# A selective scan with its sum over states: the products h*C moved between engines, and the scan written in place

## The chip, the cores and the metric

The kernel runs on one core of one Trainium2 chip. The metric is the device time of one execution in microseconds (us), from the first to the last instruction; the time of a kernel is the median of several runs. The engines are TensorE (PE, with its weight loads as PEld), VectorE (DVE), ScalarE (ACT), GpSimd (POOL), and SyncE (SP), which issues the transfers. Each has its own queue of instructions, and they meet at semaphores.

## The reference

Eight images of 56 x 56 tokens with 192 channels go through two layers, each added to its input. The first layer is a group norm, depthwise convolutions for q, k and v, and softmax attention with three heads. The second is a group norm and a selective scan in four directions (along rows, along columns, and both reversed). The change touches the scan alone:

```python
delta = jax.nn.softplus(dts + dt_projs_bias[None, :, :, None])

def step(h, inp):
    u_l, d_l, B_l, C_l = inp
    dA = jnp.exp(d_l[..., None] * A)
    dBu = d_l[..., None] * B_l[:, :, None, :] * u_l[..., None]
    h = dA * h + dBu
    y = jnp.sum(h * C_l[:, :, None, :], axis=-1)
    return (h, y)
...
_, ys = jax.lax.scan(step, h0, inputs)
```

For each image and direction the scan runs over 3136 tokens. It has 384 channels (Din), and each channel has 16 states, each with its own A, B and C. B and C belong to a token and a state and are the same for all channels. y sums h*C over the 16 states.

## The kernel before

A direction is cut into 7 chunks of T = 448 tokens, so that there are 8 x 4 x 7 = 224 chunks, each with 16 states. The channels lie on the 128 partitions in NJ = 3 blocks; a tile of one state and one chunk is 128 x 3 x 448. Constants and pools of buffers:

```python
BY_DVE = (0, 6, 11)
BY_POOL = (3, 8, 13)
...
    s1 = ctx.enter_context(tc.tile_pool(name="s1", bufs=1))
    s2 = ctx.enter_context(tc.tile_pool(name="s2", bufs=2))
    s3 = ctx.enter_context(tc.tile_pool(name="s3", bufs=3))
    s4 = ctx.enter_context(tc.tile_pool(name="s4", bufs=4))
    py = ctx.enter_context(tc.tile_pool(name="py", bufs=1, space=PSUM))
    pa = ctx.enter_context(tc.tile_pool(name="pa", bufs=2, space=PSUM))
    pb = ctx.enter_context(tc.tile_pool(name="pb", bufs=3, space=PSUM))
...
    def bank(name):
        return pb.tile([128, 512], F32, name=name, tag="bank")
```

The three banks of `pb` are shared by nearly all that TensorE writes, the attention and the convolutions too; `da` has two banks of its own, `y` three.

What a chunk needs ahead of its scan (delta as `dl`, delta times u as `du`, the C of each token as a column, `ct`) is prepared while the chunk before it runs:

```python
...
        pct = bank("pct")
        ct = s2.tile([TP, SUB, NST], F32, name="ct")
        nc.scalar.copy(ct, pct[:TP, :SUB * NR].rearrange("p (s r) -> p s r", r=NR)[:, :, R + NST:NR])
        st["ct"] = ct

        dl = s2.tile([128, NJ, T], F32, name="dl")
        e = s1.tile([128, NJ, T], F32, name="e")
        ln = s1.tile([128, NJ, T], F32, name="ln")
        for j in range(NJ):
            pdt = bank("pdt")
            nc.tensor.matmul(pdt[:, :T], dtws[k][:, j * 128:(j + 1) * 128], xd[0:R, :], start=True, stop=True)
            q = k * NJ + j
            nc.scalar.activation(e[:, j], pdt[:, :T], AF.Abs, bias=dtb[:, q])
            nc.scalar.activation(dl[:, j], pdt[:, :T], AF.Relu, bias=dtb[:, q])
            yield st
        nc.scalar.activation(e, e, AF.Exp, scale=-1.0)
        nc.scalar.activation(ln, e, AF.Identity, bias=one)
        nc.vector.scalar_tensor_tensor(e, ln, -1.0, e, ALU.add, ALU.subtract)
        nc.scalar.activation(ln, ln, AF.Ln)
        nc.vector.tensor_tensor(dl, dl, e, ALU.subtract)
        nc.vector.tensor_tensor(dl, dl, ln, ALU.add)
        du = s2.tile([128, NJ, T], F32, name="du")
        nc.gpsimd.tensor_tensor(du, dl, xs, ALU.mult)
        st["dl"], st["du"] = dl, du
        yield st
```

The loop over the states of a chunk:

```python
        y = py.tile([128, NJ, 512], F32, name="y")
        newc = s2.tile([128, NJ, NST], F32, name="newc")
        done = []
        for n in range(NST + 1):
            if n < NST:
                bb = s4.tile([128, T], F32, name="bb")
                nc.sync.dma_start(bb, rows[n, :].partition_broadcast(128))
                cm = None
                if n in BY_DVE:
                    cm = bank("cm")
                    nc.tensor.matmul(cm[:, :T], sel[:, BY_DVE.index(n), :], xd, start=True, stop=True)
                elif n in BY_POOL:
                    cm = s2.tile([128, T], F32, name="cb")
                    nc.sync.dma_start(cm, rows[NST + n, :].partition_broadcast(128))
                dbu = s3.tile([128, NJ, T], F32, name="dbu")
                nc.gpsimd.tensor_tensor(
                    dbu, du, bb.unsqueeze(1).to_broadcast([128, NJ, T]), ALU.mult)
                h = s4.tile([128, NJ, T], F32, name="h")
                for j in range(NJ):
                    da = pa.tile([128, 512], F32, name="da")
                    nc.scalar.activation(da[:, :T], dl[:, j], AF.Exp,
                                         scale=acoef[:, k * NJ + j, n:n + 1])
                    nc.vector.tensor_tensor_scan(
                        h[:, j, rev], da[:, 0:T][:, rev], dbu[:, j, rev],
                        0.0 if ci == 0 else carry[:, j, n:n + 1], ALU.mult, ALU.add)
                nc.scalar.copy(newc[:, :, n:n + 1], h[:, :, last])
                done.append((n, h, cm))
            if n >= 1:
...
```

`dbu` is delta*u*B by GpSimd; `da` is exp(delta*A) by ScalarE, in a PSUM bank; VectorE scans along the tokens, three instructions a state, from `da` and `dbu` into `h`; ScalarE copies the last column for the next chunk. Then h*C is added to `y` in one of three ways:

```python
    def add_state(n, h, cm, y, ct):

        if n in BY_DVE:
            nc.vector.tensor_tensor(h, h, cm[:, :T].unsqueeze(1).to_broadcast([128, NJ, T]), ALU.mult)
        elif n in BY_POOL:
            for j in range(NJ):
                nc.gpsimd.tensor_tensor(h[:, j], h[:, j], cm, ALU.mult)
        if n in BY_DVE or n in BY_POOL:
            for j in range(NJ):
                nc.tensor.matmul(y[:, j, :T], ident, h[:, j], start=(n == 0), stop=(n == NST - 1))
            return

        for s in range(SUB):
            cols = slice(s * TP, (s + 1) * TP)
            ht = bank("ht")
            for j in range(NJ):
                nc.tensor.transpose(ht[:TP, j * 128:(j + 1) * 128], h[:, j, cols], ident)
            g = s3.tile([TP, DIN], F32, name="g")
            nc.scalar.activation(g, ht[:TP, :DIN], AF.Copy, scale=ct[:, s, n:n + 1])
            for j in range(NJ):
                nc.tensor.matmul(y[:, j, cols], g[:, j * 128:(j + 1) * 128], ident[:TP, :TP],
                                 is_transpose=True, start=False, stop=(n == NST - 1 and s == SUB - 1))
```

States 0, 6 and 11: VectorE multiplies by C, which TensorE has spread over the partitions (`cm`), and TensorE adds to `y` by a matmul with the identity. States 3, 8 and 13: GpSimd multiplies, by C rows that a transfer has spread (`cb`). The ten others: TensorE transposes blocks of 112 tokens to a bank `ht`, so that C lies along the partitions and is a scale of a ScalarE copy (`g`), and transposes back, adding in `y`.

Between the states the loop interleaves other work: `finish`, the output projection of the image before, in the chunks of direction 0; and `front`, the first layer and the second layer's convolution of the image to come, in the chunks of directions 1 to 3 (in all four for the first image). The last image has no front beside its scan.

```python
...
                slot += 1
                want = total * (slot - first_slot) / (NTOK - NST - first_slot)
                while spent < want:
                    got = next(fill, None)
                    if got is None:
                        break
                    spent += got
...
```

The program's instructions are put in a fixed order for each engine when it is built: a scheduler sets the order, by what is ready and by the program's own sequence.

Of the kernel before, what the change touches and what calls it, by code (L numbers as in the profile page):

```python
# [8 lines left out]
F32 = mybir.dt.float32  # L9
AF = mybir.ActivationFunctionType  # L10
ALU = mybir.AluOpType
# [10 lines left out]
T = 448  # L22
# [12 lines left out]
NJ = DIN // 128  # L35
NST = 16
R = 12
NR = R + 2 * NST
NDIR = 4
BY_DVE = (0, 6, 11)  # L40
BY_POOL = (3, 8, 13)
EPS = 1e-5
CAP = 60.0
NTOK = NDIR * NCH * NST
# [3 lines left out]
def kernel(  # L48
# [24 lines left out]
    nc = tc.nc  # L73
# [7 lines left out]
    def fill(name, shape, value):  # L81
        t = const.tile(shape, F32, name=name)
        nc.vector.memset(t, value)
        return t
# [5 lines left out]
    one = fill("one", [128, 1], 1.0)  # L90

    heads2 = fill("heads2", [128, 2, TP], 0.0)
    for h in range(2):
# [7 lines left out]
                            base=0, pattern=[[-6, 16], [0, 6]], channel_multiplier=1)  # L101
    nc.gpsimd.affine_select(out=gv, in_=gv, compare_op=ALU.is_ge, fill=0.0,
                            base=5, pattern=[[6, 16], [0, 6]], channel_multiplier=-1)


    sel = fill("sel", [NR, len(BY_DVE), 128], 1.0)
    for i, n in enumerate(BY_DVE):
        nc.gpsimd.affine_select(out=sel[:, i], in_=sel[:, i], compare_op=ALU.is_equal, fill=0.0,
                                base=-(R + NST + n), pattern=[[0, 128]], channel_multiplier=1)

    pwq = load("pwq", [CP, NB, C], pw_q.rearrange("(b p) d -> p b d", p=CP))
    pwkv = load("pwkv", [CP, NB, 2 * C], pw_kv.rearrange("(b p) d -> p b d", p=CP))
# [59 lines left out]
    s1 = ctx.enter_context(tc.tile_pool(name="s1", bufs=1))  # L172
    s2 = ctx.enter_context(tc.tile_pool(name="s2", bufs=2))
    s3 = ctx.enter_context(tc.tile_pool(name="s3", bufs=3))
    s4 = ctx.enter_context(tc.tile_pool(name="s4", bufs=4))
    py = ctx.enter_context(tc.tile_pool(name="py", bufs=1, space=PSUM))
    pa = ctx.enter_context(tc.tile_pool(name="pa", bufs=2, space=PSUM))
    pb = ctx.enter_context(tc.tile_pool(name="pb", bufs=3, space=PSUM))
# [2 lines left out]
    def bank(name):  # L181
        return pb.tile([128, 512], F32, name=name, tag="bank")
# [359 lines left out]
    def prepare(b, k, c, i):  # L542

        xs = s2.tile([128, NJ, T], F32, name="xs")
        nc.sync.dma_start(xs, made[b]["xcs"][k % 2][:, :, c * T:(c + 1) * T])
        if i == 0:
            dtw = s2.tile([R, DIN], F32, name="dtw")
            nc.sync.dma_start(dtw, dt_wT[:, k, :])
            dtws[k] = dtw
        yield {}  # L550
        px = bank("px")
        for j in range(NJ):
            nc.tensor.matmul(px[:NR, :T], xpw[:, k, j], xs[:, j], start=(j == 0), stop=(j == NJ - 1))
        xd = s2.tile([NR, T], F32, name="xd")
        nc.scalar.copy(xd, px[:NR, :T])
        rows = dchunk.tile([2 * NST, T], F32, name="rows")
        nc.sync.dma_start(rows, xd[R:NR, :])
        st = {"xs": xs, "xd": xd, "rows": rows}
# [4 lines that stand above are left out]
            nc.tensor.transpose(pct[:TP, s * NR:(s + 1) * NR], xd[:, s * TP:(s + 1) * TP], ident[:NR, :NR])  # L563
# [3 lines that stand above are left out]

        dl = s2.tile([128, NJ, T], F32, name="dl")
        e = s1.tile([128, NJ, T], F32, name="e")
        ln = s1.tile([128, NJ, T], F32, name="ln")  # L570
        for j in range(NJ):
            pdt = bank("pdt")
            nc.tensor.matmul(pdt[:, :T], dtws[k][:, j * 128:(j + 1) * 128], xd[0:R, :], start=True, stop=True)  # L573
            q = k * NJ + j
            nc.scalar.activation(e[:, j], pdt[:, :T], AF.Abs, bias=dtb[:, q])
            nc.scalar.activation(dl[:, j], pdt[:, :T], AF.Relu, bias=dtb[:, q])  # L576
            yield st
        nc.scalar.activation(e, e, AF.Exp, scale=-1.0)
        nc.scalar.activation(ln, e, AF.Identity, bias=one)
        nc.vector.scalar_tensor_tensor(e, ln, -1.0, e, ALU.add, ALU.subtract)  # L580
        nc.scalar.activation(ln, ln, AF.Ln)
        nc.vector.tensor_tensor(dl, dl, e, ALU.subtract)
        nc.vector.tensor_tensor(dl, dl, ln, ALU.add)  # L583
        du = s2.tile([128, NJ, T], F32, name="du")
        nc.gpsimd.tensor_tensor(du, dl, xs, ALU.mult)  # L585
        st["dl"], st["du"] = dl, du
        yield st

    def run_all(gen):
        st = None  # L590
        for st in gen:
            pass
        return st

    def add_state(n, h, cm, y, ct):

        if n in BY_DVE:
            nc.vector.tensor_tensor(h, h, cm[:, :T].unsqueeze(1).to_broadcast([128, NJ, T]), ALU.mult)  # L598
        elif n in BY_POOL:
            for j in range(NJ):  # L600
                nc.gpsimd.tensor_tensor(h[:, j], h[:, j], cm, ALU.mult)  # L601
        if n in BY_DVE or n in BY_POOL:
            for j in range(NJ):
                nc.tensor.matmul(y[:, j, :T], ident, h[:, j], start=(n == 0), stop=(n == NST - 1))  # L604
            return
# [13 lines that stand above are left out]
    total = sum(front(0))  # L619
    cur = run_all(prepare(*steps[0]))  # L620
    carry = None
    fill, spent, given = None, 0.0, 0
    es = None
    for i, (b, k, c, ci) in enumerate(steps):
        if k == 0 and ci == 0:
# [3 lines left out]
            fill = front(b + 1) if b + 1 < nb else iter(())  # L629
# [3 lines left out]
        nxt = None  # L633
        rev = slice(None, None, -1 if k >= 2 else 1)
        last = slice(0, 1) if k >= 2 else slice(T - 1, T)
        dl, du, xd, rows, ct, xs = (cur[v] for v in ("dl", "du", "xd", "rows", "ct", "xs"))
        y = py.tile([128, NJ, 512], F32, name="y")
        newc = s2.tile([128, NJ, NST], F32, name="newc")
        done = []
        for n in range(NST + 1):  # L640
            if n < NST:
                bb = s4.tile([128, T], F32, name="bb")
                nc.sync.dma_start(bb, rows[n, :].partition_broadcast(128))
                cm = None
                if n in BY_DVE:
                    cm = bank("cm")
                    nc.tensor.matmul(cm[:, :T], sel[:, BY_DVE.index(n), :], xd, start=True, stop=True)  # L647
                elif n in BY_POOL:
                    cm = s2.tile([128, T], F32, name="cb")
                    nc.sync.dma_start(cm, rows[NST + n, :].partition_broadcast(128))  # L650
                dbu = s3.tile([128, NJ, T], F32, name="dbu")
                nc.gpsimd.tensor_tensor(  # L652
                    dbu, du, bb.unsqueeze(1).to_broadcast([128, NJ, T]), ALU.mult)
                h = s4.tile([128, NJ, T], F32, name="h")
                for j in range(NJ):
                    da = pa.tile([128, 512], F32, name="da")
                    nc.scalar.activation(da[:, :T], dl[:, j], AF.Exp,  # L657
                                         scale=acoef[:, k * NJ + j, n:n + 1])
                    nc.vector.tensor_tensor_scan(  # L659
                        h[:, j, rev], da[:, 0:T][:, rev], dbu[:, j, rev],  # L660
                        0.0 if ci == 0 else carry[:, j, n:n + 1], ALU.mult, ALU.add)
                nc.scalar.copy(newc[:, :, n:n + 1], h[:, :, last])  # L662
                done.append((n, h, cm))
            if n >= 1:
                add_state(*done[n - 1], y, ct)
            if n >= 2 and n % 2 == 0:
                nxt = next(ahead, nxt)
            if n < NST:
                for _ in range(2):
                    next(ending, None)  # L670
# [7 lines that stand above are left out]
# [16 lines left out]
        carry, cur = newc, nxt  # L694
# [63 lines left out]
```

## Time and profile before

| what | value |
|---|---|
| time, median of 3 runs | 21997.85 us (21988.34 to 22036.88) |
| span of the profiled run | 21990.5 us |
| TensorE, busy share | 86% |
| VectorE, busy share | 70% |
| ScalarE, busy share | 66% |
| GpSimd, busy share | 66% |
| mean granted TensorE clock | 0.92 |

The profile page lists groups of instructions by line of the kernel: the line, engine and operation, what is written and what is read, the shapes, the count, then the busy time in us and the mean duration of one in ns, and after the bar the idle time of the engine just before them with what ended most of it. The view of waits lists pairs: who waited for whom, us in total, how often, and the longest. The view of stretches gives for a part of the trace its length and, for each engine, the busy us and the count. A busy share is an average over the whole span, and matmuls that follow each other overlap in it.

### The profile page before, as it was taken

What the parts mean: (1) busy time and instruction counts of PE and PEld (TensorE: products, weight loads), DVE (VectorE), ACT (ScalarE), POOL (GpSimd) and SP (SyncE); (2) the same over time, 40 slices, a digit from 0 to 9 for tenths busy, and PEclk for the clock granted to TensorE, in tenths of its full rate; (3) what the DMA queues carried; (4) which work ended last, traced back from release to release, by engine and by line L of the source; (5) the groups of instructions that cost most, each with busy time, mean ns of one, the idle gap of its engine ahead of it and who ended that gap; (6) DMA issues with size and microseconds to landing.
All of it is one profiled execution on the core that took longest, in us unless ns stands there. A gap on an engine that the chain in (4) does not pass through costs nothing. (4 is left out here: it accounts for less than half of the span.)

```text
span 21990.5 us, 246125 instructions
## 1 busy us (share of the span) xinstructions
PE 18854.4 (86%) x84640; PEld 11005.3 (50%) x84640; DVE 15390.6 (70%) x14585; ACT 14548.1 (66%) x28166; POOL 14468.7 (66%) x6131
## 2 busy tenths in 40 slices
PE   8889888899888998889888899888988889887776
PEld 4454555545455455554555545555455554554444
DVE  1477777766677666876677766777667776677775
ACT  2467667666675766757666676666767667677665
POOL 0467677666676667766677666776667666677775
PEclk9899999999999999999999999999999999998888
DMA  1222222222222222222223222222222222222221
GB/s 50 82 66 66 67 84 65 74 62 65 82 68 71 63 69 77 81 61 61 73 75 80 60 62 73 76 77 62 61 84 68 76 61 61 81 70 67 61 61 41
DMA packets 935285, 1508.59 MB, mean 69 GB/s; under 512 B 102480, under 2 KB 917904, under 8 KB 930960
## 3 DMA queue, kind: packets, MB, share of 16 engines
q1 hardware_dynamic: 934032, 1492.83, 24.3%
q8 instruction: 670, 10.98, 0.2%
q14 instruction: 583, 4.78, 0.1%
HBM read 1322.38 MB, written 170.08 MB: 68 GB/s over the span
## 5 line engine op out<-in xcount | busy, mean ns | idle before, releaser
L652 POOL TENSOR_TENSOR dbu<-du,bb 128x1344 f32<-128x1344 f32 x3584 | 10845.1, 3040 | 4585.7 <-DVE h L659 2376.8
L659 DVE TENSOR_TENSOR_SCAN h<-da,newc,dbu 128x448 f32<-128x448 f32 x9216 | 10006.9, 1134 | 4142.2 <-PE ht L611 1467.0
L657 ACT ACTIVATE da<-dl,acoef 128x448 f32<-128x448 f32 x10752 | 6795.8, 638 | 3454.9 <-DVE h L659 3423.1
L613 ACT ACTIVATE g<-ht,ct 112x384 f32<-112x384 f32 x8960 | 4786.1, 576 | 1364.1 <-PE ht L611 1331.2
L615 PE MATMUL y<-ident,g 112*128 112x112 f32 x26880 | 4360.3, 281 | 1316.2 <-ACT g L613 1276.1
L611 PE MATMUL ht<-ident,h 128*112 128x128 f32 x26880 | 4483.0, 288 | 671.5 <-DVE h L659 182.1
L615 PEld LDWEIGHTS y<-ident,g 112*128 112x128 f32 x26880 | 2994.2, 147 | 3629.3 <-ACT g L613 3017.1
L604 PE MATMUL y<-h,ident 128*128 128x448 f32 x8064 | 3805.4, 611 | 473.2 <-DVE h L598 207.5
L611 PEld LDWEIGHTS ht<-ident,h 128*112 128x112 f32 x26880 | 3213.5, 141 | 1978.7 <-issue 1012.7
L601 POOL TENSOR_TENSOR h<-h,cb 128x448 f32<-128x448 f32 x2016 | 2508.1, 1272 | 1374.7 <-ACT newc L662 1374.7
L604 PEld LDWEIGHTS y<-h,ident 128*128 128x128 f32 x8064 | 1588.3, 211 | 2092.7 <-issue 1472.4
L659 DVE TENSOR_TENSOR_SCAN h<-da,dbu 128x448 f32<-128x448 f32 x1536 | 1579.6, 1072 | 676.2 <-PE ht L611 209.2
L662 ACT COPY newc<-h 128x3 f32<-128x3 f32 x3584 | 702.9, 196 | 1267.6 <-DVE h L659 1260.8
L215 PE MATMUL pcv<-xa,dg 128*128 128x440 f32 (+2 forms) x3024 | 1303.0, 545 | 0.3 <-ACT g L613 0.3
L388 PE MATMUL ps<-qT,kT 64*112 64x448 f32 x2352 | 1160.3, 605 | 70.3 <-DMA qT<-qd 38.3
L598 DVE TENSOR_TENSOR h<-h,cm 128x1344 f32<-128x1344 f32 x672 | 1035.9, 1542 | 255.8 <-PE cm L647 244.2
L396 PE MATMUL po<-pT,vt 112*128 112x448 f32 x2352 | 1043.1, 550 | 0.0
L585 POOL TENSOR_TENSOR du<-dl,xs 128x1344 f32<-128x1344 f32 x224 | 679.8, 3035 | 540.6 <-DVE dl L583 526.2
L391 ACT ACTIVATE pT<-ps,nsh 112x448 f32<-112x448 f32 x1176 | 726.1, 630 | 290.9 <-PE ps L388 237.8
L215 PE MATMUL pq<-band,dgq 96*96 96x440 f32 (+3 forms) x2016 | 866.4, 546 | 0.0
L647 PE MATMUL cm<-xd,sel 44*128 44x448 f32 x1344 | 712.0, 611 | 6.5 <-ACT dl L576 6.5
L573 PE MATMUL pdt<-xd,dtw 12*128 12x448 f32 x1344 | 708.0, 607 | 0.0
(140 smaller groups left out, 12929.0 us busy)
## 6 DMA issues: line engine op xcount, KB each, us to landing
bb<-rows SPq DMA_DIRECT2D x3584, 224.0 KB
cb<-rows SPq DMA_DIRECT2D x672, 224.0 KB
xt<-x1d SPq DMA_DIRECT2D x224, 336.0 KB
xs<-xch SPq DMA_DIRECT2D x112, 672.0 KB
xs<-xcw SPq DMA_DIRECT2D x112, 672.0 KB
xch<-xv SPq DMA_DIRECT2D x24, 1568.0 KB
xcw<-xw SPq DMA_DIRECT2D x168, 224.0 KB
xin<-in_x_dram SPq DMA_DIRECT2D x56, 336.0 KB
```

The lines of the kernel that those rows point to most:

```text
L215: nc.tensor.matmul(out[:, o0:o1, a:b], lhs, img(lo, hi)[:, :, a + dx - 1:b + dx - 1], start=(t == TAPS[0]), stop=(t == TAPS[-1]))
L388: nc.tensor.matmul(ps[:TP, :T], kh[rows, kb * TP:(kb + 1) * TP], qh[rows, :], start=True, stop=True)
L396: nc.tensor.matmul(po[:, :T], vt[:, kb, g:g + 2, :].rearrange("p g d -> p (g d)"), pts[kb], start=(kb == 0), stop=(kb == NKB - 1))
L598: nc.vector.tensor_tensor(h, h, cm[:, :T].unsqueeze(1).to_broadcast([128, NJ, T]), ALU.mult)
L601: nc.gpsimd.tensor_tensor(h[:, j], h[:, j], cm, ALU.mult)
L604: nc.tensor.matmul(y[:, j, :T], ident, h[:, j], start=(n == 0), stop=(n == NST - 1))
L611: nc.tensor.transpose(ht[:TP, j * 128:(j + 1) * 128], h[:, j, cols], ident)
L613: nc.scalar.activation(g, ht[:TP, :DIN], AF.Copy, scale=ct[:, s, n:n + 1])
L615: nc.tensor.matmul(y[:, j, cols], g[:, j * 128:(j + 1) * 128], ident[:TP, :TP], is_transpose=True, start=False, stop=(n == NST - 1 and s = ...
L652: nc.gpsimd.tensor_tensor(dbu, du, bb.unsqueeze(1).to_broadcast([128, NJ, T]), ALU.mult)
L657: nc.scalar.activation(da[:, :T], dl[:, j], AF.Exp, scale=acoef[:, k * NJ + j, n:n + 1])
L659: nc.vector.tensor_tensor_scan(h[:, j, rev], da[:, 0:T][:, rev], dbu[:, j, rev], 0.0 if ci == 0 else carry[:, j, n:n + 1], ALU.mult, ALU.add)
```

## The change

The states that VectorE multiplied now go over the transposed blocks, with ScalarE, so that 13 states go this way and GpSimd keeps three, now 0, 5 and 10. With that `cm`, its matmuls and its selection matrix are gone. The scan is written in place: GpSimd puts delta*u*B into the tile `h`, and VectorE scans that tile into itself. Three tiles `dbu` and four tiles `h` become eight tiles `h`. The room for the eighth comes from the tile `ln`, whose part `du` plays until it gets its own value. The purpose is to unload VectorE and to let the engines run further apart.

```diff
@@ -37,8 +37,7 @@
 R = 12
 NR = R + 2 * NST
 NDIR = 4
-BY_DVE = (0, 6, 11)
-BY_POOL = (3, 8, 13)
+BY_POOL = (0, 5, 10)
 EPS = 1e-5
 CAP = 60.0
 NTOK = NDIR * NCH * NST
@@ -102,12 +101,6 @@
     nc.gpsimd.affine_select(out=gv, in_=gv, compare_op=ALU.is_ge, fill=0.0,
                             base=5, pattern=[[6, 16], [0, 6]], channel_multiplier=-1)
 
-
-    sel = fill("sel", [NR, len(BY_DVE), 128], 1.0)
-    for i, n in enumerate(BY_DVE):
-        nc.gpsimd.affine_select(out=sel[:, i], in_=sel[:, i], compare_op=ALU.is_equal, fill=0.0,
-                                base=-(R + NST + n), pattern=[[0, 128]], channel_multiplier=1)
-
     pwq = load("pwq", [CP, NB, C], pw_q.rearrange("(b p) d -> p b d", p=CP))
     pwkv = load("pwkv", [CP, NB, 2 * C], pw_kv.rearrange("(b p) d -> p b d", p=CP))
     outw0 = load("outw0", [128, C], out_w[0:128, :])
@@ -173,6 +166,7 @@
     s2 = ctx.enter_context(tc.tile_pool(name="s2", bufs=2))
     s3 = ctx.enter_context(tc.tile_pool(name="s3", bufs=3))
     s4 = ctx.enter_context(tc.tile_pool(name="s4", bufs=4))
+    s8 = ctx.enter_context(tc.tile_pool(name="s8", bufs=8))
     py = ctx.enter_context(tc.tile_pool(name="py", bufs=1, space=PSUM))
     pa = ctx.enter_context(tc.tile_pool(name="pa", bufs=2, space=PSUM))
     pb = ctx.enter_context(tc.tile_pool(name="pb", bufs=3, space=PSUM))
@@ -567,7 +561,7 @@
 
         dl = s2.tile([128, NJ, T], F32, name="dl")
         e = s1.tile([128, NJ, T], F32, name="e")
-        ln = s1.tile([128, NJ, T], F32, name="ln")
+        du = s2.tile([128, NJ, T], F32, name="du")
         for j in range(NJ):
             pdt = bank("pdt")
             nc.tensor.matmul(pdt[:, :T], dtws[k][:, j * 128:(j + 1) * 128], xd[0:R, :], start=True, stop=True)
@@ -576,12 +570,11 @@
             nc.scalar.activation(dl[:, j], pdt[:, :T], AF.Relu, bias=dtb[:, q])
             yield st
         nc.scalar.activation(e, e, AF.Exp, scale=-1.0)
-        nc.scalar.activation(ln, e, AF.Identity, bias=one)
-        nc.vector.scalar_tensor_tensor(e, ln, -1.0, e, ALU.add, ALU.subtract)
-        nc.scalar.activation(ln, ln, AF.Ln)
+        nc.scalar.activation(du, e, AF.Identity, bias=one)
+        nc.vector.scalar_tensor_tensor(e, du, -1.0, e, ALU.add, ALU.subtract)
+        nc.scalar.activation(du, du, AF.Ln)
         nc.vector.tensor_tensor(dl, dl, e, ALU.subtract)
-        nc.vector.tensor_tensor(dl, dl, ln, ALU.add)
-        du = s2.tile([128, NJ, T], F32, name="du")
+        nc.vector.tensor_tensor(dl, dl, du, ALU.add)
         nc.gpsimd.tensor_tensor(du, dl, xs, ALU.mult)
         st["dl"], st["du"] = dl, du
         yield st
@@ -594,12 +587,9 @@
 
     def add_state(n, h, cm, y, ct):
 
-        if n in BY_DVE:
-            nc.vector.tensor_tensor(h, h, cm[:, :T].unsqueeze(1).to_broadcast([128, NJ, T]), ALU.mult)
-        elif n in BY_POOL:
+        if n in BY_POOL:
             for j in range(NJ):
                 nc.gpsimd.tensor_tensor(h[:, j], h[:, j], cm, ALU.mult)
-        if n in BY_DVE or n in BY_POOL:
             for j in range(NJ):
                 nc.tensor.matmul(y[:, j, :T], ident, h[:, j], start=(n == 0), stop=(n == NST - 1))
             return
@@ -633,7 +623,7 @@
         nxt = None
         rev = slice(None, None, -1 if k >= 2 else 1)
         last = slice(0, 1) if k >= 2 else slice(T - 1, T)
-        dl, du, xd, rows, ct, xs = (cur[v] for v in ("dl", "du", "xd", "rows", "ct", "xs"))
+        dl, du, rows, ct, xs = (cur[v] for v in ("dl", "du", "rows", "ct", "xs"))
         y = py.tile([128, NJ, 512], F32, name="y")
         newc = s2.tile([128, NJ, NST], F32, name="newc")
         done = []
@@ -642,22 +632,18 @@
                 bb = s4.tile([128, T], F32, name="bb")
                 nc.sync.dma_start(bb, rows[n, :].partition_broadcast(128))
                 cm = None
-                if n in BY_DVE:
-                    cm = bank("cm")
-                    nc.tensor.matmul(cm[:, :T], sel[:, BY_DVE.index(n), :], xd, start=True, stop=True)
-                elif n in BY_POOL:
+                if n in BY_POOL:
                     cm = s2.tile([128, T], F32, name="cb")
                     nc.sync.dma_start(cm, rows[NST + n, :].partition_broadcast(128))
-                dbu = s3.tile([128, NJ, T], F32, name="dbu")
+                h = s8.tile([128, NJ, T], F32, name="h")
                 nc.gpsimd.tensor_tensor(
-                    dbu, du, bb.unsqueeze(1).to_broadcast([128, NJ, T]), ALU.mult)
-                h = s4.tile([128, NJ, T], F32, name="h")
+                    h, du, bb.unsqueeze(1).to_broadcast([128, NJ, T]), ALU.mult)
                 for j in range(NJ):
                     da = pa.tile([128, 512], F32, name="da")
                     nc.scalar.activation(da[:, :T], dl[:, j], AF.Exp,
                                          scale=acoef[:, k * NJ + j, n:n + 1])
                     nc.vector.tensor_tensor_scan(
-                        h[:, j, rev], da[:, 0:T][:, rev], dbu[:, j, rev],
+                        h[:, j, rev], da[:, 0:T][:, rev], h[:, j, rev],
                         0.0 if ci == 0 else carry[:, j, n:n + 1], ALU.mult, ALU.add)
                 nc.scalar.copy(newc[:, :, n:n + 1], h[:, :, last])
                 done.append((n, h, cm))
```

## The prediction

> **What bounds the kernel now.** I read the page's busy times first, then the costliest groups, then the waits, and last stretches of the trace with and without the convolution and attention work of the next image.
>
> The groups of the scan, from the page (the count, then busy us, then mean ns of one, then idle time just before and who ended it):
>
> ```profile
> PE 18854.4 (86%) x84640; PEld 11005.3 (50%) x84640; DVE 15390.6 (70%) x14585; ACT 14548.1 (66%) x28166; POOL 14468.7 (66%) x6131
> ...
> L652 POOL TENSOR_TENSOR dbu<-du,bb 128x1344 f32<-128x1344 f32 x3584 | 10845.1, 3040 | 4585.7 <-DVE h L659 2376.8
> L659 DVE TENSOR_TENSOR_SCAN h<-da,newc,dbu 128x448 f32<-128x448 f32 x9216 | 10006.9, 1134 | 4142.2 <-PE ht L611 1467.0
> L657 ACT ACTIVATE da<-dl,acoef 128x448 f32<-128x448 f32 x10752 | 6795.8, 638 | 3454.9 <-DVE h L659 3423.1
> L613 ACT ACTIVATE g<-ht,ct 112x384 f32<-112x384 f32 x8960 | 4786.1, 576 | 1364.1 <-PE ht L611 1331.2
> L615 PE MATMUL y<-ident,g 112*128 112x112 f32 x26880 | 4360.3, 281 | 1316.2 <-ACT g L613 1276.1
> L611 PE MATMUL ht<-ident,h 128*112 128x128 f32 x26880 | 4483.0, 288 | 671.5 <-DVE h L659 182.1
> ...
> L604 PE MATMUL y<-h,ident 128*128 128x448 f32 x8064 | 3805.4, 611 | 473.2 <-DVE h L598 207.5
> ...
> L601 POOL TENSOR_TENSOR h<-h,cb 128x448 f32<-128x448 f32 x2016 | 2508.1, 1272 | 1374.7 <-ACT newc L662 1374.7
> ...
> L598 DVE TENSOR_TENSOR h<-h,cm 128x1344 f32<-128x1344 f32 x672 | 1035.9, 1542 | 255.8 <-PE cm L647 244.2
> ```
>
> No engine is full, and each waits for another. The unit to count in is the chunk (448 tokens of one direction, 16 states): 224 of them, 3584 states. The view of waits shows the loop:
>
> ```profile
> ACT da L657 <- DVE h L659: 3423.1, 4200, 7.1
> ...
> DVE h L659 <- PE ht L611: 1676.1, 750, 8.9
> ...
> POOL h L601 <- ACT newc L662: 1374.7, 196, 17.7
> DVE h L659 <- ACT da L657: 1358.8, 1098, 8.7
> ACT g L613 <- PE ht L611: 1331.2, 1527, 10.4
> PE y L615 <- ACT g L613: 1276.1, 1563, 6.6
> ...
> DVE h L659 <- PE y L604: 833.0, 391, 8.4
> ```
>
> Read it as a circle. The scan waits for one of four h tiles, which TensorE frees (1676 + 833 us). ScalarE, blocked at da, waits for the scan; the g copies behind it in its queue are late; TensorE waits for g, and so frees h late.
>
> Two kinds of chunk must be kept apart. The times between successive du multiplies (one per chunk) give 154 chunks of 97.5 us mean, in which the front of an image is interleaved, 69 without it at about 86 us (20 of them, the last image's later directions, almost all at 85.3), and 1034 us of start and end: 154 x 97.5 + 69 x 86.1 + 1034 = 21,990. Stretches of the first kind (650 us) and of the second (one chunk), columns busy us and count of PE, weight load, DVE, ACT, POOL, then granted clock, DMA:
>
> ```profile
> 4780.00:5430.00 650.00, 598.22 (x2474) 323.58 (x2472) 438.42 (x413) 454.24 (x882) 405.92 (x170) 0.93 0.24 64
> 20356.00:20441.00 85.00, 62.74 (x298) 37.35 (x298) 65.21 (x56) 57.68 (x115) 61.17 (x26) 0.84 0.21 61
> ```
>
> With the front, TensorE is 92% busy in that stretch; without it nothing exceeds 77%, so those 85 us are a ring of waits and not a full engine. In one such chunk VectorE stands idle 20 us: 8.4 us where the profile names no releaser and the dbu tile was late, 10.8 us for da.
>
> **What the Trainium skill says.** "Perfetto Trace Analysis", section Identifying the Most-Contended Engine: matmul occupancy overstates how full TensorE is, as matmuls are pipelined. The trace agrees: one transpose lasts 273 ns, but six in a row take 0.82 us, so (0.82 - 0.27) / 5 = 0.11 us apart. "TensorE: Matmul & The Clock Gate", section Architectural detail: TensorE can pull weight loads ahead but keeps matmuls in order, and ScalarE and VectorE are strict first-in-first-out. The circle above needs just that, and one place shows it: VectorE sat 4.54 us at 20572 for da, while ScalarE sat 2.73 us ahead of its xd copy, whose matmul came after six matmuls of a GpSimd state that took 4.22 us. "GPSIMD Engine Reference", section Specifications: GpSimd shares its SBUF interface with VectorE instructions that read two SBUF tensors. The trace fits: the e subtraction (L580) beside a GpSimd multiply took 4.39 us, against 1.53 us elsewhere. The VectorE multiply that is removed reads one operand from PSUM, so I book no relief for GpSimd from it. The same trace page's Optimization Strategy takes recurring gaps as a possible sign of too few buffers; the h waits above are such gaps.
>
> **The change, part by part, per chunk.**
>
> VectorE: three multiplies go, 3 x 1.54 = -4.6 us. The scans remain, 48 x about 1.13 = 54 us. From 65.2 to 60.6 us without front.
>
> ScalarE: three states more with four g copies each, 12 x 0.576 = +6.9 us. From 57.7 to 64.6 without front; with front a mean of 64.9 becomes about 72 of 97.5. ScalarE becomes the second fullest engine, but not full.
>
> TensorE: a VectorE state cost six y matmuls and two cm matmuls. Spacing in runs: six y take 2.43 us with the last lasting 0.54, so 0.38 each; the two cm stand 0.48 apart. 6 x 0.38 + 2 x 0.48 = 3.2 us. A transposed state costs 12 transposes at 0.11 and 12 back at 0.10 (six take 0.79, the last 0.28): 2.5 us. By spacing, 3 x -0.7 = -2.1 us a chunk. By busy time it is (4483.0 + 4360.3) / 2240 = 3.95 us against 3805.4 / 1344 + 712.0 / 672 = 3.89, so nothing. The truth lies between, and how well the short transposes are fed decides it. Each transposed state has also cost 1276 / 2240 = 0.57 us of TensorE waiting for g: three more, +1.7 us if the circle turned as before.
>
> GpSimd: still three states' multiplies and 16 dbu's. Count and bytes are unchanged, and the transfer of C rows (cb) is three per chunk as before. Nothing in busy time.
>
> Banks: cm no longer holds one of three PSUM banks that ht, the attention scores and the convolutions share. It was written before the scan and held till the VectorE multiply. That helps ht run ahead.
>
> Buffers: three dbu and four h tiles become eight tiles for both. A dbu may now be made while TensorE is up to eight states behind, instead of the scan stopping at four. The 2509 us of scan waits for h (16 us for each of the 154 chunks with front work, where nearly all of them are) should nearly go, and GpSimd, which waited 2377 us for a dbu tile, can run ahead, filling the 6.5 us hole that the profile shows before du. Writing in place changes nothing in the length of a scan.
>
> The waits removed are not all on the path. With the front, TensorE has 85.6 us busy on average of 97.5: the most to be won is some 12 us, and the 1.7 us and ScalarE's 6.9 us work against it. I take a little over a third: 97.5 -> 93. Without the front, VectorE's 4.6 us fall out and part of the 20 us of idle with it; ScalarE at 64.6 us becomes the fullest. It was at 57.7 of 85.3, so I take 79: ScalarE 82% full, a figure chosen between 75 (the GpSimd-to-scan hand-over alone, five states of 3.04 + 3.3 for the multiply + 1.4 waiting, about 20 us, x 3.2 = 64, plus the du part of some 10) and 85. Sum: 1034 + 154 x 93 + 69 x 79 = 1034 + 14,322 + 5,451 = 20,807 us. I say 20,850, 5.2% less.
>
> **The rivals.**
>
> First, ScalarE takes VectorE's place. It gains 224 x 6.9 = 1548 us, more than the 1036 us VectorE loses, and its g copies stand in one queue with the da that the scan needs. If each g is on the path, the chunk loses the 4.6 us and gains 6.9: +2.3 x 224 = +520, about 22,500. For it: ACT da waits behind ht today. Against: ScalarE was idle 28 us in the plain chunk, waiting for the scan for most of it.
>
> Second, TensorE is the bound wherever the front runs, and the new order feeds it no better. Then the 154 chunks stay at 97.5 and only the 69 move, by 7: 21,500, 2% less. For it: 92% busy in that stretch. Against: 0.11 us spacing in place of 0.27 shows that much of the busy time is tails.
>
> Third, state 0 moves from VectorE to GpSimd. It opens the accumulation in y, so a chunk's first y matmul now waits 3.3 us of multiplies where it waited 1.5, and GpSimd stands for newc before it (1375 us already). Two to four us in each chunk would give back 450 to 900 us: about 21,500. More tiles in hand speak against it, as the scan is ahead of TensorE at the seam.
>
> Fourth, the ring frees everything, 90 and 75: 20,070.
>
> **Range and chances.** From the fourth rival to half of the first: 20,000 to 21,950. Two per cent below before is 21,558, which the second and third rivals reach only just; two above is 22,438. Chances: faster 0.73, same 0.18, slower 0.09.
>
> **What will show it.** Right: scan waits for ht and y below 600 us together (from 2509); g groups 11,648 copies, ScalarE about 16,100 us busy; VectorE about 14,350; the plain chunk under 81 us; GpSimd's wait for the scan ahead of dbu halved; y waiting for g no longer than 1700 us. Wrong: a da wait of VectorE that grows past 2500 us (first rival), front chunks at 97 us (second), or y matmuls of state 0 waiting on GpSimd over 2 us a chunk (third). Above all it is wrong if the fixed order of instructions puts the eight tiles all on TensorE's side, so that GpSimd waits for ht instead of the scan.

## The result, and the profile after

The changed kernel takes 23480.12 us (median, 23443.43 to 23509.13), against 22007.75 us for the kernel before in the same comparison: a ratio of 1.0667 (95% interval 1.0647 to 1.0687). It is slower by 6.7%, where 5.2% less was predicted.

The page of the kernel after, engines and groups of the scan (L639 makes delta*u*B, now into `h`; L645 is the scan; L643 `da`; L601 and L605 the transposes there and back; L603 the `g` copies; L592 GpSimd's h*C; L594 its sum):

```profile
PE 18962.1 (81%) x95392; PEld 12115.5 (52%) x95392; DVE 14393.2 (61%) x13912; ACT 15790.6 (67%) x30854; POOL 14176.1 (60%) x6128
...
L645 DVE TENSOR_TENSOR_SCAN h<-da,newc,h 128x448 f32<-128x448 f32 x9216 | 10055.5, 1136 | 5114.0 <-ACT da L643 2901.0
L639 POOL TENSOR_TENSOR h<-du,bb 128x1344 f32<-128x1344 f32 x3584 | 10823.3, 3040 | 3344.3 <-PE ht L601 2298.8
L643 ACT ACTIVATE da<-dl,acoef 128x448 f32<-128x448 f32 x10752 | 6762.1, 637 | 2900.9 <-DVE h L645 2796.7
L605 PE MATMUL y<-ident,g 112*128 112x112 f32 x34944 | 5928.0, 290 | 2120.3 <-ACT g L603 2076.4
L603 ACT ACTIVATE g<-ht,ct 112x384 f32<-112x384 f32 x11648 | 6180.0, 575 | 1902.0 <-PE ht L601 1840.6
L601 PE MATMUL ht<-ident,h 128*112 128x128 f32 x34944 | 6097.4, 296 | 769.1 <-DVE h L645 168.0
...
L594 PE MATMUL y<-h,ident 128*128 128x448 f32 x4032 | 1929.7, 614 | 1058.5 <-POOL h L592 924.3
```

The work did what it was meant to. VectorE is 997 us less busy, ScalarE 1243 us more, TensorE 108 us more, and one scan lasts 1136 ns after 1134. The loss is idle time. The view of waits after (L578 makes du, L574 is a step of delta on VectorE, `e`, that waits for ScalarE's L573):

```profile
POOL du L578 <- DVE dl L577: 3404.0, 186, 36.1
DVE h L645 <- ACT da L643: 3293.7, 2382, 13.5
ACT da L643 <- DVE h L645: 2796.7, 2783, 13.0
DVE h L645 <- POOL h L639: 2501.7, 662, 7.5
POOL h L639 <- PE ht L601: 2298.8, 726, 15.5
PE y L605 <- ACT g L603: 2076.4, 1825, 12.9
...
DVE e L574 <- ACT du L573: 1449.0, 222, 21.2
```

and two lines of the same view before:

```profile
POOL du L585 <- DVE dl L583: 526.2, 117, 11.4
...
DVE e L580 <- ACT ln L579: 303.0, 154, 3.4
```

Before, the scan waited 2509 us for TensorE to free a tile and 452 us for its delta*u*B. Now it waits 8 us for TensorE and 2502 us for delta*u*B, and GpSimd waits 2299 + 582 = 2880 us for TensorE (ht, and y for its own states). This wait has not gone; it has moved one engine back. It is not the whole loss, however: the scan's two tile waits together even fell, from 2961 to 2510 us, while VectorE's idle time grew by 2484 us. What grew are its waits for ScalarE: for da from 1359 to 3294 us, and before `e` from 303 to 1449 us.

By chunk (from one du multiply to the next) the time is lost in two of three places. "Front" are the 154 chunks with the first layer beside them, "direction 0" the 49 with the output projection, "plain" the 20 of the last image. The last two columns are us in the view of waits.

| kernel | ratio (95% interval) | front | direction 0 | plain | scan for delta*u*B | GpSimd for TensorE |
|---|---|---|---|---|---|---|
| before | 1 | 97.5 | 86.8 | 84.2 | 452 | 556 |
| after | 1.0667 (1.0647-1.0687) | 103.1 | 98.9 | 85.9 | 2502 | 2880 |
| e1 ring only | 1.0775 (1.0755-1.0796) | 107.0 | 92.8 | 81.8 | 3295 | 2842 |
| e2 states only | 0.9752 (0.9732-0.9771) | 93.8 | 88.9 | 80.9 | 408 | 308 |
| e3 after, GpSimd 3, 8, 13 | 1.0603 (1.0583-1.0623) | 103.7 | 93.3 | 85.8 | 2790 | 2312 |
| e4 after, order pinned | 1.0650 (1.0626-1.0673) | 103.2 | 96.7 | 87.9 | 3069 | 2505 |
| e5 dbu 3, h 5 | 0.9881 (0.9866-0.9896) | 95.6 | 89.1 | 81.1 | 878 | 247 |
| e6 dbu 4, h 4 | 0.9785 (0.9770-0.9800) | 94.5 | 89.3 | 80.3 | 417 | 293 |
| e7 ring of six | 1.1027 (1.1010-1.1043) | 111.0 | 92.6 | 80.5 | 5626 | 5405 |
| e8 as e2, GpSimd 3, 8, 13 | 0.9957 (0.9941-0.9974) | 96.3 | 88.4 | 84.6 | 430 | 499 |
| e9 ring, a third of the multiply | 0.9784 (0.9769-0.9799) | 95.0 | 87.9 | 78.1 | 1620 | 6023 |
| e10 two rings, a third | 0.9555 (0.9539-0.9570) | 92.4 | 86.1 | 76.2 | 779 | 680 |
| e11 e2 and VectorE's load | 1.0357 (1.0341-1.0373) | 98.3 | 99.6 | 84.1 | 319 | 334 |
| e12 e2, two GpSimd states | 0.9808 (0.9793-0.9822) | 94.1 | 89.1 | 83.1 | 240 | 337 |
| e13 ring, multiply split | 1.0481 (1.0464-1.0499) | 99.2 | 100.9 | 88.7 | 1833 | 1894 |
| e14 two rings, split | 0.9701 (0.9686-0.9716) | 93.7 | 87.1 | 78.8 | 666 | 41 |

Inside the front chunks of the changed kernel the time without a scan has gathered at the seam, between a chunk's last scan and the first of the next. Means over the 154, in us; pdt is the matmul with which TensorE begins the delta of the next chunk:

| kernel | first scan to last scan | last scan to the next chunk's first | the next chunk's last pdt matmul ends |
|---|---|---|---|
| before | 95.9 | 1.8 | 18.7 before the last scan ends |
| e2 states only | 91.9 | 1.8 | 16.9 before |
| e5 dbu 3, h 5 | 90.3 | 5.3 | 12.7 before |
| after | 81.5 | 21.6 | 5.8 after it |
| e7 ring of six | 100.9 | 10.1 | 7.9 before |
| e9 ring, a third of the multiply | 75.1 | 19.9 | 5.9 after it |
| e13 ring, multiply split | 79.5 | 19.7 | 5.6 after it |

The scan does run ahead of TensorE in the changed kernel, and gets through its 16 states sooner. But the delta of the next chunk comes through TensorE, which is behind by then; from pdt over ScalarE, VectorE and du to the next scan there pass some 16 us more, and no scan runs: the hole of 21.6 us. Of VectorE's 1449 us before `e` 1293 lie in this hole, and of GpSimd's 3404 us before du 1782. TensorE is idle for only 1.4 us of its 21.6: it works off the states that it was behind. So what the scan wins inside the chunk, it gives back at the seam.

### The profile page after: what moved, and what is told of

Read it like the earlier page. It is cut to its first block, busy times and chain, and to the rows that moved or that the text cites. A ratio compares the mean times of both kernels' runs of the same rounds, so it can differ in the third digit from the quotient of the medians.

```text
span 23477.6 us, 275529 instructions
## 1 busy us (share of the span) xinstructions
PE 18962.1 (81%) x95392; PEld 12115.5 (52%) x95392; DVE 14393.2 (61%) x13912; ACT 15790.6 (67%) x30854; POOL 14176.1 (60%) x6128
## 5 line engine op out<-in xcount | busy, mean ns | idle before, releaser
L645 DVE TENSOR_TENSOR_SCAN h<-da,newc,h 128x448 f32<-128x448 f32 x9216 | 10055.5, 1136 | 5114.0 <-ACT da L643 2901.0
L639 POOL TENSOR_TENSOR h<-du,bb 128x1344 f32<-128x1344 f32 x3584 | 10823.3, 3040 | 3344.3 <-PE ht L601 2298.8
L643 ACT ACTIVATE da<-dl,acoef 128x448 f32<-128x448 f32 x10752 | 6762.1, 637 | 2900.9 <-DVE h L645 2796.7
L605 PE MATMUL y<-ident,g 112*128 112x112 f32 x34944 | 5928.0, 290 | 2120.3 <-ACT g L603 2076.4
L603 ACT ACTIVATE g<-ht,ct 112x384 f32<-112x384 f32 x11648 | 6180.0, 575 | 1902.0 <-PE ht L601 1840.6
L601 PE MATMUL ht<-ident,h 128*112 128x128 f32 x34944 | 6097.4, 296 | 769.1 <-DVE h L645 168.0
L605 PEld LDWEIGHTS y<-ident,g 112*128 112x128 f32 x34944 | 4139.3, 154 | 4824.7 <-ACT g L603 4184.7
L601 PEld LDWEIGHTS ht<-ident,h 128*112 128x112 f32 x34944 | 4378.6, 145 | 1996.0 <-issue 819.5
L578 POOL TENSOR_TENSOR du<-dl,xs 128x1344 f32<-128x1344 f32 x224 | 679.5, 3034 | 4179.5 <-DVE dl L577 3404.0
L594 PE MATMUL y<-h,ident 128*128 128x448 f32 x4032 | 1929.7, 614 | 1058.5 <-POOL h L592 924.3
L592 POOL TENSOR_TENSOR h<-h,cb 128x448 f32<-128x448 f32 x2016 | 2237.2, 1139 | 682.4 <-ACT newc L648 681.9
L645 DVE TENSOR_TENSOR_SCAN h<-da,h 128x448 f32<-128x448 f32 x1536 | 1586.1, 1074 | 839.3 <-POOL h L639 430.4
L594 PEld LDWEIGHTS y<-h,ident 128*128 128x128 f32 x4032 | 788.7, 211 | 1929.8 <-POOL h L592 1177.6
L574 DVE SCALAR_TENSOR_TENSOR e<-du,e 128x1344 f32<-128x1344 f32 x224 | 349.1, 1558 | 1449.0 <-ACT du L573 1449.0
```

Source lines behind the costliest of these rows:

```text
L639: nc.gpsimd.tensor_tensor(h, du, bb.unsqueeze(1).to_broadcast([128, NJ, T]), ALU.mult)
L643: nc.scalar.activation(da[:, :T], dl[:, j], AF.Exp, scale=acoef[:, k * NJ + j, n:n + 1])
L645: nc.vector.tensor_tensor_scan(h[:, j, rev], da[:, 0:T][:, rev], h[:, j, rev], 0.0 if ci == 0 else carry[:, j, n:n + 1], ALU.mult, ALU.add)
```

## The experiments

**The two halves of the change, apart.** Theory A: GpSimd makes many delta*u*B tiles ahead of the multiply of state 0, which opens y. Theory B: ScalarE is the new bound. Theory C: the ring is at fault.

e1, the kernel before with this alone:

```diff
-                dbu = s3.tile([128, NJ, T], F32, name="dbu")
+                h = s8.tile([128, NJ, T], F32, name="h")
...
-                h = s4.tile([128, NJ, T], F32, name="h")
```

(with it the multiply writes `h`, the scan reads `h`, and `du` plays the part of `ln`).

> The kernel before, with the scan in place over eight tiles, and the states divided as before (VectorE 0, 6, 11; GpSimd 3, 8, 13). Theory A (GpSimd's fixed order puts up to eight delta*u*B multiplies ahead of the multiply of state 0, which opens y, and everything stands until it is done): state 0 is VectorE's here, so no such stand; 21,300 to 22,000 us. Theory B (ScalarE takes VectorE's place through 6.9 us a chunk of g copies): nothing added on ScalarE, 21,300 to 22,000 as well. Theory C (the ring itself, GpSimd now waiting for TensorE to free h): 23,000 us or more.

e2, the kernel before with this alone:

```diff
-BY_DVE = (0, 6, 11)
-BY_POOL = (3, 8, 13)
+BY_DVE = ()
+BY_POOL = (0, 5, 10)
```

> The kernel before, with its own three dbu and four h tiles, and only the states moved (GpSimd 0, 5, 10; thirteen over ScalarE). Theory A: GpSimd can be at most three dbu ahead of the scan, so that the multiply of state 0 comes some 9 us late at most; 22,200 to 22,900 us. Theory B: 23,200 us or more, as all ScalarE work is there. Theory C: 21,700 to 22,100 us.

e1 measured 23693.79 us, e2 21439.96 us. The whole ScalarE load is in e2, and it is 2.5% faster than before: theory B falls, and with it the first rival of the prediction. The ring alone costs 7.7%, so theory C stands (e2 came out faster still than C's range). 1.0775 x 0.9752 = 1.051; the two together cost 1.067, so some 1.6 points are from their meeting.

e3 and e4 ask what is left of theory A. e3 is the changed kernel with GpSimd's states moved:

```diff
-BY_POOL = (0, 5, 10)
+BY_POOL = (3, 8, 13)
...
-                                 is_transpose=True, start=False, stop=(n == NST - 1 and s == SUB - 1))
+                                 is_transpose=True, start=(n == 0 and s == 0),
+                                 stop=(n == NST - 1 and s == SUB - 1))
```

> The changed kernel with GpSimd's three states at 3, 8 and 13, as in the kernel before; state 0 goes over the transposed blocks, which then open y. Theory A: no GpSimd multiply opens y; 20,800 to 21,900 us, and the plain chunk falls from 85.4 to some 74 to 79 us. Theories B and C: ScalarE's load and the ring are as in the changed kernel, so 23,200 us or more.

e4 fixes one place in GpSimd's order:

```diff
-                nc.gpsimd.tensor_tensor(
+                made_b = nc.gpsimd.tensor_tensor(
                     h, du, bb.unsqueeze(1).to_broadcast([128, NJ, T]), ALU.mult)
+                if n == 2:
+                    tc.keep_in_program_order(made_b)
```

> The changed kernel with one order fixed on GpSimd: the multiply that makes delta*u*B of state 2 stands behind the three multiplies of state 0, so that two and not eight of them come ahead. Work, tiles and states are those of the changed kernel. Theory A: the stand of 10 to 12 us at a chunk's start falls to 3 to 5; 21,400 to 22,400 us. Theories B and C: unchanged, 23,200 to 23,700 us.

They measured 23306.09 and 23417.48 us: theory A alone does not explain the loss. But in direction 0 it is plain to see. GpSimd of the changed kernel, one such chunk:

```profile
12337.78 3.02 POOL L578 TENSOR_TENSOR du<-dl,xs 128x1344 f32<-128x1344 f32 x1 [14.95 <-DVE dl L577]
12340.88 23.98 POOL L639 TENSOR_TENSOR h<-du,bb 128x1344 f32<-128x1344 f32 x8
12364.83 3.29 POOL L592 TENSOR_TENSOR h<-h,cb 128x448 f32<-128x448 f32 x3
```

and in the same chunk TensorE, ScalarE and VectorE:

```profile
12366.00 4.84 PE L594 MATMUL y<-h,ident 128*128 128x448 f32 x6 [11.48 <-POOL h L592]
```

```profile
12371.58 1.05 ACT L603 ACTIVATE g<-ht,ct 112x384 f32<-112x384 f32 x2 [11.83 <-PE ht L601]
```

```profile
12373.20 1.15 DVE L645 TENSOR_TENSOR_SCAN h<-da,newc,h 128x448 f32<-128x448 f32 x1 [11.60 <-ACT da L643]
```

Eight multiplies stand in the queue ahead of the three that y waits for, and three engines stand in turn. From the end of state 0's scan to the start of its h*C there pass on average 12.0 us in the 49 chunks of direction 0 after the change, against 3.1 us in e2, where three dbu tiles let only four multiplies go ahead. Over these kernels with the same states the direction 0 chunk follows that delay: 0.3 us (e9) 87.9; 3.1 (e2) 88.9; 6.3 (e7) 92.6; 12.0 (after) 98.9; 14.5 (e13) 100.9. Only e4 does not: its delay is 0.4 us, and it stays at 96.7. GpSimd then stands 6 us for newc with the scan waiting behind it, and makes ten tiles in one stretch, beside which one VectorE step of the output projection is slow (below). Pinning the order trades one wait for others.

**What in the ring costs.** Theory D: with one ring, a tile that TensorE frees must first pass through a 3 us multiply on GpSimd before a scan may use it, so that GpSimd stands in the circle of waits; with two rings it works ahead. Theory E: eight tiles let the scan run too far ahead. Theory F: du in the part of ln. e5, with eight tiles and du in the part of ln as in the changed kernel, differs from it by this:

```diff
-                h = s8.tile([128, NJ, T], F32, name="h")
+                dbu = s3.tile([128, NJ, T], F32, name="dbu")
...
+                h = s4.tile([128, NJ, T], F32, name="h", bufs=5)
```

> The changed kernel's states and its eight tiles, and du in the part of ln, but not in place: three tiles dbu and five tiles h. In e1 and the changed kernel about 5.5 of the eight tiles stand scanned and not yet summed, and the scan finds only some 0.5 delta*u*B tiles ahead. Theory D (in one ring a delta*u*B multiply of 3 us on GpSimd has to fit between TensorE's release of a tile and the next scan, and so stands in the circle of waits): with a ring of its own GpSimd works ahead again; 20,900 to 21,600 us. Theory E (eight tiles let the scan run too far ahead of TensorE, whatever the ring): 22,300 us or more. Theory F (du in the part of ln delays the chain that makes delta): 22,500 us or more.

e6 has `bufs=4` for both.

> As e5, but four tiles dbu and four tiles h. Theory D: 21,200 to 21,700 us, near e2, as the tiles that the scan waits for are four as there. Theory E: near e2 too. Theory F: 22,500 us or more.

e7 is the changed kernel with fewer tiles:

```diff
-tc.tile_pool(name="s8", bufs=8)
+tc.tile_pool(name="s8", bufs=6)
```

> The changed kernel with six tiles in place of eight, still in place. Theory D: GpSimd waits for TensorE sooner and more often; 24,000 us or more. Theory E: the scan gets less far ahead, so faster; 22,000 to 23,000 us. Theory F: unchanged, 23,300 to 23,600 us.

e8 is e2 with `BY_POOL = (3, 8, 13)` and the start flag of e3.

> As e2 (three dbu, four h, thirteen states over ScalarE), with GpSimd's states at 3, 8 and 13 and state 0 opening y from the transposed blocks. What the place of GpSimd's states is worth in two rings: by theory D little, 21,200 to 21,700 us; by theory A (a GpSimd state that opens y holds all up) 20,700 to 21,200 us.

e5 measured 21734.97 us (a little over D's range), e6 21517.73, e7 24263.75, e8 21900.81 us. The same eight tiles in two rings save 1745 us; theory F falls with e5 and e6. Theory E, as it was put, falls with e7, which is slower and not faster. A part of it is true all the same: with six tiles the hole at the seam shrinks from 21.6 to 10.1 us, but the states before it take 100.9 us in place of 81.5; and e5, with a fifth h tile in place of e6's fourth dbu, costs 217 us more. Theory A fails in e8, which is slower than e2; e8 lies above D's range too, so that the place of GpSimd's states is worth more in two rings than D said. The waits of e7, as the dose is raised:

```profile
DVE h L645 <- POOL h L639: 5625.5, 1445, 8.6
...
POOL h L639 <- PE ht L601: 4678.2, 1229, 11.6
```

and of e2, two rings:

```profile
DVE h L655 <- PE ht L607: 2266.6, 890, 8.0
...
POOL dbu L648 <- DVE h L655: 1983.5, 858, 14.6
```

In e2 GpSimd waits because it is ahead of the scan, and the scan takes a freed tile at once. In e7 each wait for TensorE is answered by one for GpSimd. Counted at each state's first scan in the front chunks, states scanned and not yet summed are 3.4 before and 5.5 after, and finished delta*u*B tiles ahead 0.9 and 0.6: the tiles gather on TensorE's side, and few are left for working ahead.

**Length of the multiply.** e9 is the changed kernel, e10 is e5, with two thirds of the products left out:

```diff
-                    h, du, bb.unsqueeze(1).to_broadcast([128, NJ, T]), ALU.mult)
+                    h[:, 0], du[:, 0], bb, ALU.mult)
```

(dbu in e10; all three scans read block 0, in the order 1, 2, 0).

> The changed kernel (one ring of eight), with two thirds of the delta*u*B multiply left out: GpSimd makes the first of three channel blocks, 1.0 us in place of 3.04, and all three scans read it. The other two blocks' products are left out. Theory D (the multiply's length stands between TensorE's release of a tile and the next scan): most of the gap to the two rings goes; 21,000 to 22,000 us, within 3% of e10. Against D (in place costs by something else): the gap of 1,745 us between one ring and two stays at 1,300 or more, e9 at 22,700 or above.

> e5 (three dbu, five h) with the same two thirds of the multiply left out. GpSimd is hardly on the path with two rings, so 20,900 to 21,700 us by theory D. If GpSimd's work itself is what binds, 20,000 us or less.

They measured 21510.29 and 21013.01 us. The gap between one ring and two falls from 1745 to 497 us. GpSimd in e9 waits even more for TensorE (6023 us), but hands the tile on in 1.1 us. As this takes work away too, e13 keeps the work and splits it:

```diff
-                nc.gpsimd.tensor_tensor(
-                    h, du, bb.unsqueeze(1).to_broadcast([128, NJ, T]), ALU.mult)
+                for j in range(NJ):
+                    nc.gpsimd.tensor_tensor(h[:, j], du[:, j], bb, ALU.mult)
```

> The changed kernel (one ring of eight) with delta*u*B made by three GpSimd instructions of one channel block each, about 1.1 us, in place of one of 3.04. Nothing is left out; GpSimd's work rises by some 0.4 us a state. Theory D as latency: the first scan of a state can start 2 us sooner after TensorE frees its tile; 22,300 to 23,000 us, clearly below the changed kernel. If GpSimd's load and not the latency is what costs: 23,500 to 24,500 us.

e14 is the same edit in e2.

> e2 (three dbu, four h) with the same split. By theory D as latency there is little to win where GpSimd has a ring of its own: 21,200 to 21,700 us, within 1.5% of e2's 21,440. If the load costs, 21,800 us or more.

e13 measured 23046.98 us (47 over D's range), 433 us under the changed kernel though GpSimd works longer (11843 us on these products, 10823 before the split); e14 measured 21332.43 us, the fastest version with nothing left out, ratio 0.9701 (0.9686 to 0.9716). So the delay to the first scan is part of the price: front chunks fall from 103.1 to 99.2 us, by 2.0 us inside the chunk and by 1.9 at the seam, where the first multiply follows du. The rest of the gap (e9: 95.0) goes with the time of the whole multiply, which the third scan still waits for and which sets how fast GpSimd can answer several freed tiles in a row. How these two share it was not separated. Nor was the order: in all rings of eight the delta chain of the next chunk stands behind 47.6 or more of a front chunk's 48 scans in VectorE's queue, against 42.5 in e2 and 45.3 in e5, and no kernel with a ring was run with the chain placed earlier. e9 has a hole of 19.9 us too, and its front chunk takes 95.0 us, so a hole of that size need not make the chunk long where the multiply is short.

**Where e2's gain is from.** e11 is e2 with a load on VectorE:

```diff
+        if n in (1, 6, 11):
+            nc.vector.tensor_tensor(h, h, ones.unsqueeze(1).to_broadcast([128, NJ, T]), ALU.mult)
```

> e2 with VectorE given its load back: in states 1, 6 and 11 it multiplies h by ones, three instructions of some 1.5 us a chunk, ahead of the transposes; cm with its matmuls and its bank stays away. If e2 gains by VectorE's freed time, it returns to 21,800 to 22,100 us; if it gains by the bank and the matmuls that cm no longer takes, it stays within 1% of e2's 21,440.

It measured 22780.76 us, 1341 more than e2 and outside both ranges. The multiply turned out twice as long as the one it stands for; both its inputs lie in SBUF, and GpSimd was at work beside nearly all of them (the last section has the figures):

```profile
L605 DVE TENSOR_TENSOR h<-h,ones 128x1344 f32<-128x1344 f32 x672 | 2020.9, 3007 | 313.8 <-ACT newc L661 313.5
```

So each us on VectorE costs 0.66 us of time (1341 / 2021). At that rate the 1036 us that the change removes are worth about 690 us; e2 gained 563. By chunk the two agree less well. The 9 us added to a chunk cost 4.5 in the front chunks, 10.7 in direction 0 and 3.2 in the plain ones; removing 4.6 us gained 3.8 and 3.3 in the front and the plain ones, and direction 0 became 2.1 us slower. So VectorE's time is a part of the gain. That it is all of it, and that cm's bank and matmuls are worth nothing, was not shown, the less so as the added multiply also stands between a scan and its transposes.

e12 is e2 with `BY_POOL = (0, 8)`.

> e2 with only two states on GpSimd (0 and 8) and fourteen over ScalarE: a try at a faster version. GpSimd loses 3.4 us a chunk of work that stands in its queue, ScalarE gains 2.3. If ScalarE is not the bound (theory B false), 21,000 to 21,600 us; if it is, 21,800 us or more.

It measured 21564.31 us, 0.6% above e2: moving a state from GpSimd to ScalarE won nothing.

## Why the prediction was wrong

**The unloading was right.** VectorE's -4.6 us a chunk came as -4.5 (997 / 224), ScalarE's +6.9 as +5.5, TensorE's "nothing" by busy time as +0.5. The states alone, e2, give 21440 us, inside the range.

**The step that failed is the buffers.** The prediction said that the scan's 2509 us of waiting for h "should nearly go, and GpSimd, which waited 2377 us for a dbu tile, can run ahead". The scan's wait for TensorE did go, to 8 us, but as a wait for GpSimd and as the hole at the seam. I counted eight tiles against seven and a longer reach, and did not follow one tile round: before, TensorE's release led straight to a scan whose delta*u*B lay ready; after, it leads to a multiply first. "Writing in place changes nothing in the length of a scan" was true and beside the point: in place makes two stages share a ring, and the slower consumer takes most of it (5.5 of eight tiles). That the scan runs ahead was right inside the chunk (81.5 us against 95.9 before); what I left out is that the next chunk's delta comes through the engine that lags, so that the lead ends at the seam: 21.6 us without a scan, where it was 1.8. Thus the front chunks, which I put at 93, came at 103.1. The last sentence of the prediction names the ring, and I gave it no number. The front chunks hold 1434 of the 2026 us between the profiled spans of after and e2 (154 x 9.31). How this divides between the multiply in the circle and the late delta chain stays open.

**Signs that came true beside a wrong result.** The scan's wait for tiles fell below 600 us, the g copies were 11,648, and VectorE was busy 14,393 us: three of the signs for "right", and the kernel is 6.7% slower. They show that the work moved as planned and a wait left its old place; the plain chunk (85.9, not under 81) and y's wait for g (2076 us, not under 1700) told otherwise.

**The third rival was real, too small, and in other chunks.** I gave two to four us to each chunk, and the y matmul of state 0 waited 865 us for GpSimd, 3.9 us a chunk. In direction 0 the changed kernel is 9.96 us over e2 (49 x 9.96 = 488 us), in the plain ones 5.0 (100 us). I took the ring's depth as protection against a late state 0; it is what lets GpSimd's queue fill ahead of it.

**The plain chunk.** I put it at 79 and it came at 85.9; e2 gives 80.9.

**The rivals.** The first (ScalarE) is refuted by e2, though VectorE's wait for da grew to 3294 us, past the mark I had set for it: da was late as ScalarE's queue stood behind ht, and not for want of ScalarE time. So that mark did not tell the theories apart. The second held in kind: TensorE's share was no gain. (The Trainium skill's "Perfetto Trace Analysis", section Identifying the Most-Contended Engine, says only that matmul busy time is a poor measure because matmuls are pipelined; that it reads too high I took from the 0.11 us spacing in this trace.) The range's upper end was to be half of the first rival; half of its +520 us gives about 22,260 and not 21,950, and the result lies above both.

## What to carry to other kernels

Before joining two buffers in place, follow one tile round: if a producer's step comes between the last reader's release and the next use, the producer has joined the circle of waits, and a larger count does not give back the ring of its own that let it work ahead. A wait that vanishes from one pair of engines is to be looked for at the engine before, and at the next seam: a lead over a lagging engine lasts only until the next input has to come through that engine. Where a step that opens an accumulation sits on a queue that can run ahead, the depth of the ring is the length of the queue ahead of it.

## What the runs showed of the hardware that I had not expected

A GpSimd multiply in progress can hold a VectorE instruction until it ends, and several multiplies on end can hold it until the last of them ends. In e11 the 15 VectorE multiplies with both inputs in SBUF and no GpSimd instruction beside them took 1552 ns on average, and the 657 others 3040; all 592 that took over 1.65 us ended 1.42 us after a GpSimd instruction had, as if they had started only then. With one input in PSUM nothing of this is seen: before the change the multiply of that shape took 1543 ns beside GpSimd's instructions (441 times) and 1539 without. In e4, where GpSimd multiplies ten times on end, even the one-input scale and shift of the output projection took 2446 ns on average, against 572 in the changed kernel:

```profile
L494 DVE TENSOR_SCALAR yc<-yc,lnw,lnb 128x448 f32<-128x448 f32 x168 | 402.1, 2446 | 0.3
```

Of these 168, the 119 with no GpSimd instruction beside them took 503 ns, and 49 took 6.4 to 10.2 us. In the chunk of e4 that corresponds to the one above, GpSimd's run and the three steps that met it:

```profile
12338.46 29.96 POOL L639 TENSOR_TENSOR h<-du,bb 128x1344 f32<-128x1344 f32 x10
12361.90 7.61 DVE L494 TENSOR_SCALAR yc<-yc,lnw,lnb 128x448 f32<-128x448 f32 x3
```

The run ends at 12368.42, and so only the last 1.1 us of the three steps' 7.61 lie behind it.

And TensorE was granted a clock of 0.883 in the changed kernel, against 0.920 before and 0.923 in e2. Its busy time in front chunks is 86.8 us after and 82.7 in e2 for the same 95,392 matmuls in all, which is 4.1 of the 9.3 us between these chunks. Whether the lower clock or shorter runs of matmuls, with more tails, made it longer was not shown: one transpose lasts 296 ns on average after and 289 in e2.
